# Last layer of a four-layer graph network: one two-bank PSUM tile for the turned factors, one bank for the side work

## The chip, the core and the metric

The kernel runs on one core of one Trainium2 chip. The metric is the device time of one execution in microseconds, as the median of several runs. TensorE (PE), VectorE (DVE), ScalarE (ACT), GpSimd (POOL) and SyncE (SP, which here only issues transfers) run side by side, each through its own queue in order; semaphores tie them together. PE writes its results into PSUM, of which each of 128 partitions has eight banks of 512 fp32 numbers. A tile of `[128, 512]` fp32 fills one bank.

## The reference

`x` is 4096 x 64, `adj` is 4096 x 4096. Four layers follow one another, each as `x = layernorm(x + layer(x, adj, ...))`: a Chebyshev layer, an attention layer with two GRU cells, a layer with decaying weights of the last neighbours of each row, and a layer in the Poincare ball. The change lies in the last one, with the curvature 1:

```python
def _logmap(x, y, c):
    sub = _mobius_add(-x, y, c)
    sub_norm = jnp.maximum(jnp.linalg.norm(sub, axis=-1, keepdims=True), MIN_NORM)
    x2 = jnp.sum(x * x, axis=-1, keepdims=True)
    lam_x = 2.0 / jnp.maximum(1.0 - c * x2, MIN_NORM)
    sqrt_c = jnp.sqrt(c)
    arg = jnp.clip(sqrt_c * sub_norm, 0.0, TANH_CLIP)
    return 2.0 / (sqrt_c * lam_x) * jnp.arctanh(arg) * sub / sub_norm
...
deg = jnp.maximum(adj.sum(axis=1, keepdims=True), 1e-08)
w = adj / deg
log_ij = _logmap(x[:, None, :], x[None, :, :], c)
agg = jnp.einsum('ij,ijc->ic', w, log_ij)
transformed = agg @ weight + bias
return _expmap(jnp.zeros_like(transformed), transformed, c)
```

For each pair of rows i, j the layer needs one factor f(i, j), a function of the distance of the two points, by which the adjacency is multiplied before it is summed against the features. The factor is the same for (i, j) and (j, i).

## The kernel before

The 4096 rows form 8 groups of 512. Because f is symmetric, the last layer computes it only for 36 tiles of 512 x 512, `tiles = [(i, j) ...]`, ordered by group `i` along a list `seq`: the first group has 8 tiles, the next 7, and so on down to 1. The first tile of a group is its diagonal tile. The adjacency, turned, lies in DRAM as `adj_t`; for each tile SP loads `own[t]` (the block at (i, j), buffer `at_d`) and, off the diagonal, `mirrored[t]` (the block at (j, i), buffer `at_m`), three buffers each.

Each tile is done in two halves, called units: `n` counts 72 of them (`NU`), each with 2 blocks of 128 x 512, so 128 x 1024 numbers; on the diagonal the second half is only 256 columns wide a block. The loop `while n < NU + 2` is written as a pipeline over units. In step `n` it does, in this written order:

- `gather(...)` (L1665, L1677, L1673): PE sums finished blocks of an `own` and of a `mirrored` tile against the features into `sums_ps`, one bank; a group's sums are then copied to `tb`.
- `turn(...)`: PE transposes the factors of a finished tile (L1649) for its mirrored block, four transposes of 128 x 128 into one PSUM tile `post`, and DVE multiplies each such tile into a block of `mirrored[t]` (L1651). A half has two blocks, so two `post` tiles and two multiplies. Turns of one tile are spread over two steps. A diagonal tile is turned onto itself (L1642, L1644), written at the end of its step (`late_turns`).
- ACT takes a logarithm (L1837) and an exponential (L1838) of unit `n`, the square of unit `n+1` (L1606), another exponential (L1864) and a logarithm of unit `n-1` (L1873). PE adds the sign part, `opposite(n + 1)` (L1616).
- DVE forms `f` for unit `n-2` (L1847) and multiplies it into `own` (L1850), then the multiplies of `turn`, then `rt` of unit `n` out of the product's PSUM banks (L1862), then `less_one(n + 1)` (L1627).
- PE forms `product(n + 2)` (L1594) into the two banks that L1862 has just read. Even units use pool `ps_v`, odd ones `ps_u`, two banks each.
- One step of `seam`: side work cut into pieces. At first it ends the layer before (`summed` L1389, `prepare`, `turn_prepared`); later it ends a finished group (`finals`): `first` forms products with `tb` (L1757), read by DVE (L1759) and ACT (L1767); `second` forms others (L1730), read by DVE (L1771); then normalisation and the store.
- `right(ps_p, i)`: PE forms the right side of a new group's products in two ways (L1356), four matmuls each into a `post` tile, and ACT copies each out (L1359). The second group's right side is formed at step 0; each later one six steps before the group's first unit, both ways in one step, into one of two buffers in turn.

All `post` tiles of the layer, those of `turn`, `seam` and `right`, come from one pool, `ps_p3`, of three banks. With the two banks each of `ps_v` and `ps_u` and the one of `sums_ps` that makes all eight.

What orders the work: a scheduler places each engine's instructions by the order in which they are written and by when their inputs are expected; an instruction may be drawn forward past others that wait. `in_order(ins)` forbids this for one instruction: it stays behind the instruction written just before it on its engine. The matmuls of `gather`, `opposite` and `product` are held in this way; the transposes and the side work are not. So the last transpose of a step stays ahead of the next `opposite`, and the last side matmul of a step ahead of the next `gather`. A tile of a pool can be written again only when every reader of its bank's former tile has ended.

Of the kernel before, what the change touches and what calls it, by code (L numbers as in the profile page):

```python
# [9 lines left out]
F32 = mybir.dt.float32  # L10
# [5 lines left out]
ALU = mybir.AluOpType  # L16
AX = mybir.AxisListType
PSUM = bass.MemoryType.PSUM
# [42 lines left out]
def gnn4_kernel(  # L61
# [21 lines left out]
    nc = tc.nc  # L83
    P = 128
# [3 lines left out]
    GW = GB * P  # L88
# [40 lines left out]
    ident = const.tile([P, P], F32, name="ident")  # L129
# [80 lines left out]
    def cols(b):  # L210
        return slice(b * P, (b + 1) * P)
# [317 lines left out]
    with tc.tile_pool(name="acc", bufs=1) as acc_p, tc.tile_pool(  # L529
        name="cols0", bufs=4  # L530
    ) as cols_p, tc.tile_pool(name="kept0", bufs=1) as kept_p, tc.tile_pool(name="diag0", bufs=2) as diag_p, tc.tile_pool(
        name="ps_t0", bufs=3, space=PSUM
    ) as ps_t, tc.tile_pool(name="ps_a0", bufs=1, space=PSUM) as ps_a, tc.tile_pool(
        name="ps_p0", bufs=2, space=PSUM
# [178 lines left out]
        for g in range(NG):  # L713
# [3 lines left out]
            for c in reversed(range(NCH)):  # L717
# [5 lines left out]
                for k in range(CB):  # L723
                    jb = c * CB + k
                    tp = ps_t.tile([P, GW], F32, name="tp", tag="tp")
# [37 lines left out]
                n = g * NCH + c  # L763
# [75 lines left out]
        due, n = [], 0  # L839
# [34 lines left out]
    tr_c = tr_x  # L874
# [9 lines left out]
    seq = turns_of[0] + turns_of[1]  # L884
# [371 lines left out]
    for signed in (False, True):  # L1256
        with cmp.Else() if signed else tc.If(all_positive > 0) as block:
            cmp = block
            with tc.tile_pool(name="cols1", bufs=3 if not signed else 2) as cols_p, tc.tile_pool(name="sign1", bufs=1) as sg, tc.tile_pool(
                name="tail1", bufs=1  # L1260
            ) as tl, tc.tile_pool(name="ps_a1", bufs=1, space=PSUM) as ps_a, tc.tile_pool(
                name="ps_p1", bufs=2, space=PSUM
# [7 lines left out]
    tr_o = some[:, 0 : N // 4].bitcast(BF16).rearrange("p (m n) -> p m n", n=P)  # L1270
# [76 lines left out]
    rights, begun = {}, {}  # L1347
    rvs = [some[:, N // 4 + q * GW : N // 4 + (q + 1) * GW] for q in range(2)]
    ros = [wq_signed.rearrange("p q h -> p (q h)")[:, 0 : GW // 2].bitcast(BF16)]

    def right(ps_p, i):
        q = seq.index(i) % 2
        for to, w, t in ((rvs[q], to_right, tr_c), (ros[q], to_other, tr_o)):
            ps = ps_p.tile([P, GW], F32, name="post", tag="post")
            for b in range(GB):
                nc.tensor.matmul(  # L1356
                    ps[:, cols(b)], lhsT=w[:, b % 2, :], rhs=t[:, (i * GB + b) // 2, :], start=True, stop=True
                )
            nc.scalar.copy(to, ps)  # L1359
        rights[i] = rvs[q], ros[q]  # L1360
# [65 lines left out]
    with tc.tile_pool(name="mask2", bufs=3) as mk_p, tc.tile_pool(name="wt2", bufs=3) as wt_p, tc.tile_pool(  # L1426
        name="ps_c2", bufs=1, space=PSUM
# [28 lines left out]
        gathers = []  # L1456
        busy = True
        for turn, groups in enumerate(turns_of):
            cnt = [ps_c.tile([P, GW], F32, name=f"cnt_ps{a}") for a in range(2)]
            if turn:  # L1460
                acc = [ps_a.tile([P, GW], F32, name=f"acc_ps{q}") for q in range(QG)]
                to_right, to_other, spread, wh_x = constants3()
# [5 lines left out]
            for h in reversed(range(2 * NB)):  # L1468
                jb, odd = divmod(h, 2)
                c, k = divmod(jb, CB)  # L1470
# [66 lines left out]


    with tc.tile_pool(name="ps_v3", bufs=1, space=PSUM) as ps_v, tc.tile_pool(
        name="ps_p3", bufs=3, space=PSUM  # L1540
    ) as ps_p, tc.tile_pool(name="ps_u3", bufs=1, space=PSUM) as ps_u, tc.tile_pool(name="o3", bufs=1) as op, tc.tile_pool(name="cols3", bufs=3) as cols_p, tc.tile_pool(
        name="w3", bufs=4
    ) as wp3, tc.tile_pool(name="el3", bufs=3) as el, tc.tile_pool(name="f3", bufs=2) as fp, tc.tile_pool(
        name="r3", bufs=2
    ) as rp, tc.tile_pool(
        name="ps_a3", bufs=1, space=PSUM
    ) as ps_a:
        HB = CB // 2
# [6 lines left out]
        tiles = [(i, j) for n, i in enumerate(seq) for j in seq[n:]]  # L1555
        NT = len(tiles)
        own, mirrored = {}, {}
# [4 lines left out]
        def load_own(t):  # L1562
            if t < NT and t not in own:
                i, j = tiles[t]
                own[t] = cols_p.tile([P, CB, GW], F32, name="at_d", tag="atd")
                nc.sync.dma_start(own[t], adj_t[i][:, j * CB : (j + 1) * CB, :])

        def load_mirrored(t):
            if t < NT and t not in mirrored and tiles[t][0] != tiles[t][1]:
                i, j = tiles[t]  # L1570
                mirrored[t] = cols_p.tile([P, CB, GW], F32, name="at_m", tag="atm")
                nc.sync.dma_start(mirrored[t], adj_t[j][:, i * CB : (i + 1) * CB, :])

        def columns(n):

            i, j = tiles[n // 2]
            return slice(2 * P if i == j and n % 2 else 0, GW)

        sums, fs = {}, {}
        ros.append(op.tile([P, GW], BF16, name="ro1"))  # L1580
        vs, ws, rts = {}, {}, {}
        NU = 2 * NT
# [18 lines left out]
        def square(n):  # L1601
            if n >= NU:
                return
            ws[n] = wp3.tile([P, HB, GW], F32, name="w3")
            cs = columns(n)
            nc.scalar.activation(ws[n][:, :, cs], vs[n][:, :, cs], AF.Square)  # L1606
# [26 lines left out]
        def turn(n):  # L1633

            t, h = n
            i, j = tiles[t]
            work = []
            if i == j:
                tp = ps_p.tile([P, GW], F32, name="post", tag="post")
                for k in range(HB):  # L1640
                    for b in range(HB):
                        nc.tensor.transpose(tp[:, cols(HB * k + b)], fs[t][:, b, cols(HB + k)], ident)  # L1642
                to = own[t][:, HB:CB, 0 : HB * P]
                work.append(lambda: nc.vector.tensor_tensor(to, tp.rearrange("p (k i) -> p k i", k=HB), to, ALU.mult))  # L1644
                return work
            for b in (HB * h, HB * h + 1):
                tp = ps_p.tile([P, GW], F32, name="post", tag="post")
                for k in range(CB):
                    nc.tensor.transpose(tp[:, cols(k)], fs[t][:, k, cols(b)], ident)  # L1649
                to = mirrored[t][:, b, :]  # L1650
                work.append(lambda to=to, tp=tp: nc.vector.tensor_tensor(to, tp, to, ALU.mult))  # L1651
            return work

        def gather(t, h, tm):
# [78 lines left out]
        def ahead_of_last(g):  # L1733
            def step(ps_p):
                turned_x[g] = rp.tile([P, GB, F], F32, name="xw")
                nc.scalar.copy(turned_x[g], weighed_x(ps_p, g))
                zs[g] = less_last(g)

            return step
# [71 lines left out]
            return [nothing, first, second, third, fourth, fifth]  # L1811

        seam += [weights, factors]
        turns, late_turns, gathers = {}, {}, {}

        for t in range(3):
            load_own(t)
# [6 lines left out]
        n = 0  # L1824
        while n < NU + 2 or turns or gathers:
            if n % 2:
                load_own((n + 1) // 2)
                load_mirrored((n - 1) // 2)
            after = gather(*gathers.pop(n)) if n in gathers else []
            turned = [w for what in turns.pop(n, []) for w in turn(what)]  # L1830
            if n < NU:
                if n % 2 == 0:
                    fs[n // 2] = fp.tile([P, CB, GW], F32, name="f3")
                w, cs = ws[n][:, :, columns(n)], columns(n)
                rts[n] = el.tile([P, HB, GW], F32, name="rt3")
                rt = rts[n][:, :, cs]
                nc.scalar.activation(w, w, AF.Ln)  # L1837
                nc.scalar.activation(rt, w, AF.Exp, scale=0.5)  # L1838
                square(n + 1)
                opposite(n + 1)  # L1840
            if n >= 2 and n - 2 < NU:
                m = n - 2
                t, h = divmod(m, 2)
                cm = columns(m)
                hs = slice(h * HB, (h + 1) * HB)
                f, at = fs[t][:, hs, cm], own[t][:, hs, cm]
                nc.vector.scalar_tensor_tensor(  # L1847
                    f, rts.pop(m)[:, :, cm], T_MAX, ws.pop(m)[:, :, cm], ALU.min, ALU.mult
                )
                nc.vector.tensor_tensor(at, at, f, ALU.mult)  # L1850
                diagonal = tiles[t][0] == tiles[t][1]
                before = t - 1 if t and tiles[t - 1][0] != tiles[t - 1][1] else None
                gathers[n + 1] = (t, h, before)
                if diagonal and h == 0:
                    late_turns[n + 1] = (t, 0)
                if not diagonal and h == 1:
                    turns.setdefault(n + 1, []).append((t, 0))
                    turns.setdefault(n + 2, []).append((t, 1))
            for work in turned:
                work()  # L1860
            if n < NU:
                nc.vector.scalar_tensor_tensor(rt, vs[n][:, :, cs], (1.0 + V_FLOOR) * SCALE, rt, ALU.max, ALU.add)  # L1862
                product(n + 2)
                nc.scalar.activation(w, w, AF.Exp, scale=-0.5)  # L1864
            late = turn(late_turns.pop(n)) if n in late_turns else []
            for work in after:
                work()
            less_one(n + 1)
            for work in late:
                work()  # L1870
            if 0 < n <= NU:
                rt = rts[n - 1][:, :, columns(n - 1)]
                nc.scalar.activation(rt, rt, AF.Ln, scale=1.0 / SCALE)  # L1873
            if n == NU - 6:
                seam += [ahead_of_last(g) for g in seq[-2:]]
            for _ in range(2 if n == 0 else 1):
                if seam:
                    seam.pop(0)(ps_p)
            if n == 0:
                right(ps_p, seq[1])  # L1880
            if n + 6 < NU and tiles[(n + 6) // 2][0] not in rights:
                i = tiles[(n + 6) // 2][0]
                right(ps_p, i)
            n += 1

        before, last = seam[:-6], seam[-5:]
# [49 lines left out]
```

## Time and profile before

| | |
|---|---|
| median of 3 runs | 1389.8 us (1385.99 to 1391.12) |
| the profiled execution | 1390.6 us, span 1388.5 us |
| busy over the span | PE 1298.1 us, DVE 1041.6 us, ACT 807.1 us, POOL 115.0 us |
| last layer's loop | first product at 959.7 us, last gather at 1367.7 us |
| DVE multiplies of turned factors, L1651 | 112 of 128x512, 74.4 us |
| transposes for them, L1649 | 448 |
| mean granted PE clock | 0.985 of full speed |

A profile names each group of instructions by its line, engine and operation, with the tile that it writes and the tiles that it reads (`at_m<-post,at_m`), partitions x elements, and a count. `SCALAR_TENSOR_TENSOR` and `TENSOR_TENSOR` are DVE operations with one and two whole tensors beside a scalar or none. PE does an fp32 matmul in two passes, so that such a matmul shows as two records, while an fp32 transpose shows as one. "idle before" is time in which the engine stood still just ahead of the group, with what ended the wait. The share of busy time is an average over the layers, so the last layer has to be read by itself.

### The profile page before, as it was taken

How to read it: one execution, taken by the hardware profiler on the slowest of the kernel's cores; microseconds unless marked ns; L12 is line 12 of the kernel's file. 1: busy time of each engine (PE TensorE's matmuls, PEld its weight loads, DVE VectorE, ACT ScalarE, POOL GpSimd, SP SyncE). 2: the span in 40 equal slices, each digit the busy share in tenths (PEclk: the TensorE clock that was granted, in tenths of full speed). 3: DMA queues.
4: the chain of work that ended last, by engine and by line, in shares of the span. 5: the costliest groups of instructions: out<-in, count | busy, mean ns of one | idle time of the engine just before them, and what ended most of it. 6: DMA issues, size and time to landing. Idle time of an engine off the chain costs nothing.

```text
span 1388.5 us, 19040 instructions
## 1 busy us (share of the span) xinstructions
PE 1298.1 (93%) x6790; PEld 607.6 (44%) x6790; DVE 1041.6 (75%) x1952; ACT 807.1 (58%) x1345; POOL 115.0 (8%) x200
## 2 busy tenths in 40 slices
PE   7999999999999999999999999998978888989893
PEld 5656566565544334444444323333333333333341
DVE  6699989999434257787886233436999999999997
ACT  4645444444000115654423675655989999999994
POOL 3111111101123000010101000001000000000000
PEclk9999999999999999999999999999999999999997
DMA  9999999999799999999885755453344454544430
GB/s 322 398 395 415 405 412 413 416 397 392 284 386 368 391 424 363 421 366 346 310 326 179 236 184 182 139 167 127 116 182 182 155 207 180 193 156 182 156 126 11
DMA packets 108190, 382.15 MB, mean 275 GB/s; under 512 B 20276, under 2 KB 20280, under 8 KB 76472
## 3 DMA queue, kind: packets, MB, share of 16 engines
q1 hardware_dynamic: 87096, 296.17, 58.0%
q0 software_dynamic: 12736, 76.29, 13.3%
q10 hardware_dynamic: 8256, 8.39, 1.7%
q8 instruction: 56, 0.92, 0.3%
q14 instruction: 46, 0.38, 0.1%
HBM read 294.05 MB, written 85.20 MB: 273 GB/s over the span
## 4 chain that ended last, share of the span: by engine, by line
PE 59%; ACT 18%; DVE 14%; DMA 6%; issue 2%; ACTq 0%; DVEq 0%; SPq 0%
PE pass L570 7%; PE tp L727 6%; PE w_ps L570 4%; PE a_last L1186 4%; PE pass L563 4%; PE cnt_ps L1477 4%; DMA raw<-in_adj_dram 4%; PE acc_ps L1437 4%; PE a_ps L1186 4%; PE h_ps L563 3%; ACT w L1837 3%; ACT w L1606 3%; ACT rt L1838 3%; ACT rt L1873 3%; PE wide_last L1177 2%; ACT wt L1482 2%
## 5 line engine op out<-in xcount | busy, mean ns | idle before, releaser
L734 ACT COPY at<-tp 128x512 f32<-128x512 f32 x248 | 128.1, 599 | 117.9 <-issue 90.1
L1482 ACT ACTIVATE wt<-cnt_ps 128x512 uint16<-128x512 f32 x212 | 117.5, 596 | 63.6 <-PE cnt_ps L1477 61.3
L762 DVE TENSOR_REDUCE dpart<-raw 128x4 f32<-128x2048 f32 x64 | 145.4, 2273 | 4.4 <-DMA raw<-in_adj_dram 4.3
L1665 PE MATMUL sums_ps<-at_d,some 128*64 128x512 f32 x288 | 145.1, 625 | 2.8 <-ACT tb L1684 1.1
L764 DVE TENSOR_REDUCE lows<-raw 128x1 f32<-128x2048 f32 x64 | 145.4, 2272 | 0.0
L727 PE MATMUL tp<-ident,raw 128*128 128x128 f32 x1024 | 131.9, 282 | 6.5 <-DMA raw<-in_adj_dram 5.5
L727 PEld LDWEIGHTS tp<-ident,raw 128*128 128x128 f32 x1024 | 115.9, 144 | 42.8 <-issue 32.6
L1677 PE MATMUL sums_ps<-at_m,some 128*64 128x512 f32 x224 | 109.4, 610 | 0.0
L1594 PE MATMUL v_ps<-some,tr_a 64*128 64x512 f32 (+1 forms) x288 | 79.1, 626 | 22.7 <-DVE rt L1862 21.9
L570 PE MATMUL pass<-at,cheb_n 128*128 128x512 f32 x224 | 97.5, 593 | 0.5 <-DVE cheb_n L796 0.5
L570 PE MATMUL w_ps<-at,cheb_n 128*128 128x512 f32 x200 | 91.1, 598 | 0.0
L1477 PE MATMUL cnt_ps<-m,follow 128*64 128x512 fp8e4 x480 | 81.9, 391 | 5.4 <-ACT wt L1482 2.2
L1862 DVE SCALAR_TENSOR_TENSOR rt<-v_ps,rt 128x1024 f32<-128x1024 f32 x72 | 83.1, 1155 | 2.2 <-PE post L1649 1.2
L1850 DVE TENSOR_TENSOR at_d<-at_d,f 128x1024 f32<-128x1024 f32 x72 | 83.4, 1158 | 0.1
L1847 DVE SCALAR_TENSOR_TENSOR f<-rt,w 128x1024 f32<-128x1024 f32 x72 | 83.1, 1154 | 0.4 <-ACT rt L1873 0.3
L1649 PE MATMUL post<-ident,f 128*128 128x128 f32 x448 | 69.3, 284 | 8.5 <-DVE at_m L1651 4.2
L1873 ACT ACTIVATE rt<-rt 128x1024 f32<-128x1024 f32 x72 | 72.3, 1004 | 8.4 <-DVE rt L1862 8.0
L1484 DVE TENSOR_SCALAR wt<-cnt_ps 128x512 uint16<-128x512 f32 x44 | 30.4, 691 | 61.8 <-PE cnt_ps L1477 61.8
L1651 DVE TENSOR_TENSOR at_m<-post,at_m 128x512 f32<-128x512 f32 x112 | 74.4, 679 | 2.7 <-PE post L1649 2.6
L1837 ACT ACTIVATE w<-w 128x1024 f32<-128x1024 f32 x72 | 71.8, 999 | 1.7 <-DVE w L1627 1.5
L1864 ACT ACTIVATE w<-w 128x1024 f32<-128x1024 f32 x72 | 72.4, 1006 | 0.7
L1838 ACT ACTIVATE rt<-w 128x1024 f32<-128x1024 f32 x72 | 72.4, 1005 | 0.5
(425 smaller groups left out, 2270.2 us busy)
## 6 DMA issues: line engine op xcount, KB each, us to landing
at<-adj_t SPq DMA_DIRECT2D x119, 1024.0 KB, 7.8
raw<-in_adj_dram SPq DMA_DIRECT2D x64, 1024.0 KB, 12.7
adj_t<-at POOLq DMA_DIRECT2D x62, 1024.0 KB, 8.3
at_d<-adj_t SPq DMA_DIRECT2D x36, 1024.0 KB, 4.7
at_m<-adj_t SPq DMA_DIRECT2D x28, 1024.0 KB, 6.7
m<-mask_t SPq DMA_DIRECT2D x120, 128.0 KB, 2.8
m<-mask_t SPq DMA_DIRECT2D x60, 256.0 KB, 4.1
mask_t<-mask ACTq DMA_DIRECT2D x28, 256.0 KB, 7.6
```

The lines of the kernel that those rows point to most:

```text
L570: in_order(nc.tensor.matmul(ps, lhsT=cheb_n[:, jb, k : k + 2, :], rhs=rhs, start=first, stop=last))
L727: in_order(nc.tensor.transpose(tp[:, cols(b)], raw[:, b, cols(k)], ident))
L734: nc.scalar.copy(at[:, k, :], tp)
L762: in_order(nc.vector.tensor_reduce(dpart[:, g, c, :], raw, AX.X, ALU.add))
L764: in_order(nc.vector.tensor_reduce(lows[:, n : n + 1], raw.rearrange("p b j -> p (b j)"), AX.X, ALU.min))
L1186: in_order(nc.tensor.matmul(ps[q * F : (q + 1) * F, :], lhsT=nat_a[:, c * CB + k, 0:F], rhs=of[q if signed else 0][:, k, :], start=(c == 0 ...
L1477: in_order(nc.tensor.matmul(cnt[a][r * HP : (r + 1) * HP, :], lhsT=follow, rhs=chunks[c][odd][2 * a + r][:, k, :], start=(h == 2 * NB - 1) ...
L1482: in_order(nc.scalar.activation(wt[odd][a], cnt[a], AF.Relu, scale=-128.0))
L1665: in_order(nc.tensor.matmul(bank[0:F, :], lhsT=nat_c[:, j * CB + k, :], rhs=own[t][:, k, :], start=(i == j and k == 0), stop=(j == seq[-1] ...
L1837: nc.scalar.activation(w, w, AF.Ln)
L1838: nc.scalar.activation(rt, w, AF.Exp, scale=0.5)
L1873: nc.scalar.activation(rt, rt, AF.Ln, scale=1.0 / SCALE)
```

## The change

The pool `ps_p3` goes from three banks to one, and a new pool `ps_t3` of two banks is opened, with one buffer. In `turn`, the two `post` tiles of a half become one tile of `[128, 2, 512]` in that pool; the eight transposes go into it, and one multiply over 128 x 1024 takes the place of two over 128 x 512. Everything else that used `post` in this layer (diagonal turns, `seam`, `right`) now shares the one bank of `ps_p3`. `right` gets an argument that says which of its two ways to form, and in the loop the first way is formed seven steps and the second six steps before the group's first unit.

```diff
-    def right(ps_p, i):
+    def right(ps_p, i, which=(0, 1)):
         q = seq.index(i) % 2
-        for to, w, t in ((rvs[q], to_right, tr_c), (ros[q], to_other, tr_o)):
+        for to, w, t in [((rvs[q], to_right, tr_c), (ros[q], to_other, tr_o))[m] for m in which]:
             ps = ps_p.tile([P, GW], F32, name="post", tag="post")
...
-        name="ps_p3", bufs=3, space=PSUM
-    ) as ps_p, tc.tile_pool(name="ps_u3", bufs=1, space=PSUM) as ps_u, ...
+        name="ps_p3", bufs=1, space=PSUM
+    ) as ps_p, tc.tile_pool(name="ps_t3", bufs=1, space=PSUM) as ps_t, tc.tile_pool(
+        name="ps_u3", bufs=1, space=PSUM
+    ) as ps_u, ...
...
-            for b in (HB * h, HB * h + 1):
-                tp = ps_p.tile([P, GW], F32, name="post", tag="post")
+            tp = ps_t.tile([P, HB, GW], F32, name="two_turned")
+            for b in range(HB):
                 for k in range(CB):
-                    nc.tensor.transpose(tp[:, cols(k)], fs[t][:, k, cols(b)], ident)
-                to = mirrored[t][:, b, :]
-                work.append(lambda to=to, tp=tp: nc.vector.tensor_tensor(to, tp, to, ALU.mult))
+                    nc.tensor.transpose(tp[:, b, cols(k)], fs[t][:, k, cols(HB * h + b)], ident)
+            to = mirrored[t][:, HB * h : HB * h + HB, :]
+            work.append(lambda: nc.vector.tensor_tensor(to, tp, to, ALU.mult))
             return work
...
-            if n + 6 < NU and tiles[(n + 6) // 2][0] not in rights:
-                i = tiles[(n + 6) // 2][0]
-                right(ps_p, i)
+            for m, way in ((7, 0), (6, 1)):
+                if n + m < NU:
+                    i = tiles[(n + m) // 2][0]
+                    if (i, way) not in halves and i != seq[1] and i != seq[0]:
+                        halves.add((i, way))
+                        right(ps_p, i, (way,))
```

## The prediction

> **What bounds the kernel now.** The span table places the change first: everything it touches lies between the first product of the last layer (959.7 us) and the tail (from 1370 us). So I read the busy time of each engine in stretches of that layer; the columns are length, then busy time and instruction count of PE, PEld, DVE, ACT and POOL, PE clock, DMA share, GB/s.
>
> ```profile
> 1000.00:1050.00 50.00, 41.77 (x192) 16.80 (x189) 49.40 (x82) 43.68 (x49) 0.00 (x0) 0.93 0.42 161
> 1050.00:1100.00 50.00, 43.22 (x215) 18.74 (x214) 48.83 (x77) 49.04 (x72) 1.56 (x2) 1.00 0.45 165
> ...
> 1200.00:1250.00 50.00, 45.19 (x218) 18.74 (x217) 48.09 (x76) 48.97 (x74) 1.56 (x2) 1.00 0.48 180
> ...
> 1300.00:1350.00 50.00, 47.83 (x242) 21.69 (x240) 48.51 (x81) 49.76 (x82) 1.56 (x2) 1.00 0.43 154
> ```
>
> Over all seven stretches from 1000 to 1350 us DVE is busy 336.5 us and ACT 336.5 us of 350: both 96%. PE has 87% at first and 96% in the last stretch. DMA has half its time left and decides nothing here. So two engines bound the loop together, and a third joins them late, where the groups are short.
>
> Second the groups of that layer, shapes kept apart (count | busy us, mean ns | idle before):
>
> ```profile
> L1862 DVE SCALAR_TENSOR_TENSOR rt<-v_ps,rt 128x1024 f32<-128x1024 f32 x64 | 77.7, 1214 | 2.2 <-PE post L1649 1.2 <-ACT rt L1838 0.7
> L1651 DVE TENSOR_TENSOR at_m<-post,at_m 128x512 f32<-128x512 f32 x112 | 74.4, 679 | 2.7 <-PE post L1649 2.6
> L1649 PE MATMUL post<-ident,f 128*128 128x128 f32 x448 | 69.3, 284 | 8.5 <-DVE at_m L1651 4.2 <-DVE f L1847 4.1
> ```
>
> The multiplies to be joined hardly wait (2.7 us in 112); the transposes that feed them wait more. The waits of that stretch say for what (total us, times, longest):
>
> ```profile
> PE v_ps L1594 <- DVE rt L1862: 21.9, 25, 3.5
> ...
> PEld post L1649 <- DVE at_m L1651: 10.1, 18, 1.3
> ACT rt L1873 <- DVE rt L1862: 8.0, 15, 1.9
> DVE w L1627 <- ACT w L1606: 7.5, 8, 1.8
> ```
>
> PE's main pause is before a product, which needs the bank pair that `rt` (L1862) reads. That pause is where PE now does work early. The timeline at the turn of a group shows it:
>
> ```profile
> 1213.53 0.66 PE L1642 MATMUL post<-ident,f 128*128 128x128 f32 x4
> 1214.02 1.06 PE L1757 MATMUL post<-two_w,tb 128*128 128x128 f32 x8
> 1214.91 1.00 PE L1730 MATMUL post<-wh_x,tr_a 128*128 128x64 f32 x8
> 1215.42 0.68 DVE L1644 TENSOR_TENSOR at_d<-post,at_d 128x512 f32<-128x512 f32 x1
> 1215.84 1.13 PE L1594 MATMUL v_ps<-some,tr_a 64*128 64x512 f32 x4
> 1216.90 0.64 PE L1665 MATMUL sums_ps<-at_d,some 128*64 128x512 f32 x1
> 1217.09 0.90 ACT L1767 ACTIVATE v<-post,kappa 128x64 f32<-128x64 f32 x4
> ```
>
> Three side results (a diagonal tile's turn L1642, and two steps of the previous group's end, L1757 and L1730) stand in three `post` banks at once, before the first is read at 1215.42.
>
> **The change part by part.** Durations are from the profiled execution: 1390.6 us, a span of 1388.5 and 2.1 around it. It lies 0.8 us over the median of the three runs, 1389.8, to which I add the sum.
>
> *A, one multiply for two.* 112 multiplies of 128x512 become 56 of 128x1024. By busy time: 74.4 us against 56 x 1.214 = 68.0 us (the nearest row, L1862, also reads one PSUM operand of 128x1024), 6.4 us less. By starts in the timeline: two multiplies back to back take 1.28 us (at 1213.09) and one of 1024 takes 1.21 to 1.22, so 56 x 0.07 = 3.9 us less. How much reaches the end? ACT is as busy as DVE and loses no work, so what leaves DVE mostly turns into waiting on ACT; I take half of the smaller figure, **-2 us**; ends -6.4 and 0.
>
> The Trainium skill (Perfetto Trace Analysis, section Optimizing Scalar/DVE Operations) puts the fixed cost of a DVE operation on PSUM at about 125 ns and says that grouping helps when the engine is saturated; by it 56 operations fewer would be worth 7.0 us, an estimate, against the 3.9 us of the starts above. The same section says that breaking instructions up may finish work sooner where DVE is not saturated and makes other engines wait, which speaks against this change.
>
> *B, eight transposes into one double bank.* Until now a multiply could start after four transposes (a block of four is 0.66 us) and the third bank let the next four go ahead. Now a multiply needs eight (one block of eight at 1268.91 us took 1.09 us), 0.43 us more, and the next eight cannot begin until the whole multiply has ended. Behind the last of them PE holds, in its written order, the opposite product (L1616) and then the product (L1594); behind the multiply DVE holds `rt`, and the next step's gather waits for the multiply too. Because the gather already needs the multiply, transposes placed after it never wait for the bank. Upper end: the 0.43 us in full on each of 56 halves, +24 us. Lower end: the 2.6 us that DVE waits for `post` now go away, -2.6 us. The nearest row is that small wait, so I stay near it: one half in six pays, 56/6 x 0.43 = **+4 us**.
>
> *C, one bank for the side.* At the six group ends inside the loop where both side steps follow a diagonal turn, L1757 must wait until L1644 has read the bank (1216.10 at the place shown), and L1730 until the four activations at L1767 are through (1217.99). Of PE's work 1.06 + 1.00 = 2.06 us leaves a pause that exists anyway and comes later, and the first matmul of the next gather is written behind it. The six places cost at most 6 x 2.06 = 12.4 us. The two formed halves of a new right side (L1356) are now one step apart, so a step forms one of them; but for two of the six new groups the earlier half falls into the very step of a diagonal turn and L1757, the later one into that of L1730. There a block of 1.16 us and a copy of 0.58 us (L1359) line up behind the rest: 2 x 1.74 = 3.5 us. Upper end +15.9. Lower end: L1730 holds up the product by 0.35 us at the place shown (its block ends 1215.91, `rt` was free at about 1215.5); without it 6 x 0.35 = 2.1 us are gained. PE idles some 10% before 1300 us and only 4% after, so it regains part: **+5 us**, a third of the upper end. If the bank waits are hidden by that slack and the slack is gone, as after 1300 us, the part is paid in full.
>
> The same skill page, section Optimizing Tensor Performance, Matmuls, says that independent groups should rotate through different banks so that reading one overlaps forming the next; the three blocks above do so now, and read strictly the rule would put all of the upper end, +15.9 us, on the clock, which would make the sum +18 us, an estimate.
>
> *D, edges, one answer each.* The right side at step 0 now follows the DVE add of the step before it in the same bank (964.68 + 0.69 us, against a start at 964.48): 0.9 us later, hidden, since the next product waits for `rt` until 967.47. At the tail the two last groups' L1757 stand together (16 passes, 2.05 us at 1369.86); now the second waits for the first to be read (about 1371.9) and takes 1.03 us, but its reader starts only at 1373.88: 0, at most 0.5. The earlier half of the last right side overwrites a buffer whose last product is written in the same step, 1.13 us if ACT meets that copy too soon: taken as 0. The diagonal turn keeps its form. SP's and POOL's queues are passed by nothing: no DMA is moved, and `tb` and the mirrored tiles are loaded as before.
>
> Sum: -2 + 4 + 5 = +7, so 1389.8 + 7 = **1397 us**.
>
> **The rivals.**
> *The shorter DVE path wins (not slower).* If all eight transposes fit into PE's pause between a multiply and the end of the following `rt` (1.13 us net, block of eight 1.09), B and C are nothing and A counts: 1389.8 - 3.9 to 1389.8 - 6.4 = 1383.4 to 1385.9; with the lower ends of B and C, 1378.7. For it: PE waits 21.9 us before products now. Against it: at the turns of groups that pause is already used. It decides if B and C together stay below 3.9 us, 0.07 us a half.
>
> *PE's written order becomes the loop.* Where DVE takes the multiply before `rt` and the next eight transposes were not drawn forward, a step is a ring: multiply 1.21, `rt` 1.21, product 1.13, gather 1.93 (1205.58 to 1207.51), transposes 1.09, together 6.57 us. The products at 1199.82 and 1220.41 us are four steps apart, 5.15 us a step. So 1.42 us for each half it happens to; for a quarter of 56, +20, 1410 us; for all, +80. Against it: DVE may take `rt` first, and then the ring opens.
>
> *Nothing moves.* Both engines stay at 96%, the freed 4 us are lost in waits of the same size: 1388 to 1392.
>
> **How the numbers follow.** Forecast (+2 to +15 us, own range 1392 to 1405): 0.42, since its two places are seen in the rows; nothing moves 0.22; DVE path wins 0.22; ring 0.14. A measurement of this kernel tells about 0.5%, 6.9 us. Faster by more needs under 1382.9, the better part of the DVE rival's span: 0.10. Slower by more: three quarters of the forecast and the ring, 0.32 + 0.14 = 0.46. The rest, 0.44, is within. The range 1383 to 1411 leaves out 0.10 below and about 0.09 above (half of the ring, the forecast's end).
>
> **What would show it.** Right: 56 multiplies of 128x1024 near 1.21 us; DVE's share in 1050 to 1300 falls by about 1% while ACT's does not rise; waits of the L1649 transposes on the multiply grow beyond 14 us; the blocks L1757 and L1730 start after L1644 and L1767. Wrong: transposes of eight regularly standing before the product, with DVE idle before the multiply still near 3 us (DVE rival), or idle before L1862 and L1651 over 20 us (ring). The forecast fails as a whole if the work comes out in another order on PE, so that the pauses before products change in number: they are 21.9 us, three times the sum.

## The result and the profile after

The changed kernel takes 1402.6 us (median of 6 runs, 1401.04 to 1405.0) against 1390.1 us for the kernel before (6 runs, 1385.99 to 1394.09): a ratio of 1.0094, 95% interval 1.0079 to 1.011. It is slower by about 12.5 us. The profiled execution has a span of 1400.5 us.

The time is lost inside the loop of the last layer. From the first `rt` operation to the 72nd (L1862 before, L1864 after: the line numbers of the loop move by two) the profiled executions take 390.2 us (966.26 to 1356.44) and 404.4 us (964.01 to 1368.44), 14.2 us more. What follows the last one takes 32.1 us in both, and the first comes 2.3 us earlier, so nothing is lost ahead of the loop.

The busy time of each engine in stretches of the changed kernel, with the columns as before (length, then PE, PEld, DVE, ACT, POOL, PE clock, DMA share, GB/s):

```profile
1000.00:1050.00 50.00, 39.53 (x185) 15.69 (x185) 47.39 (x71) 43.44 (x48) 0.00 (x0) 0.97 0.43 168
1050.00:1100.00 50.00, 43.77 (x210) 19.97 (x210) 48.13 (x67) 46.76 (x70) 1.03 (x2) 0.97 0.43 163
...
1200.00:1250.00 50.00, 44.89 (x202) 20.30 (x202) 44.50 (x65) 44.28 (x67) 2.11 (x2) 0.90 0.44 168
...
1300.00:1350.00 50.00, 45.14 (x227) 20.32 (x226) 48.20 (x80) 48.39 (x79) 1.56 (x2) 1.00 0.41 150
sum 350.00, PE 305.74 PEld 131.34 DVE 326.32 ACT 325.98 POOL 7.85; mean PE 43.68 PEld 18.76 DVE 46.62 ACT 46.57 POOL 1.12
```

The sum over the same seven stretches of the kernel before was:

```profile
sum 350.00, PE 310.93 PEld 131.31 DVE 336.50 ACT 336.49 POOL 7.82; mean PE 44.42 PEld 18.76 DVE 48.07 ACT 48.07 POOL 1.12
```

DVE and ACT, which bound the loop together, each stand still 10 us more in these 350 us. Neither has taken the other's place: both wait. The stretch from 1200 to 1250 us is the worst, and PE's clock is lowered there to 0.90 on average, where it was 1.00 before.

The groups of the layer, shapes apart (count | busy us, mean ns | idle before):

```profile
L1864 DVE SCALAR_TENSOR_TENSOR rt<-v_ps,rt 128x1024 f32<-128x1024 f32 x64 | 78.0, 1218 | 4.8 <-ACT rt L1840 2.7 <-ACT tb L1686 1.7
...
L1653 DVE TENSOR_TENSOR at_m<-two_turned,at_m 128x1024 f32<-128x1024 f32 x56 | 68.4, 1221 | 10.7 <-PE two_turned L1651 10.3
...
L1651 PE MATMUL two_turned<-ident,f 128*128 128x128 f32 x448 | 66.2, 284 | 16.4 <-DVE at_m L1653 13.1 <-DVE f L1849 3.2
```

The joined multiplies are 6.0 us less busy than the 112 before (74.4), but DVE waits 10.7 us ahead of them, 8.0 us more. The waits of the loop, in us in total, times and longest:

```profile
PEld two_turned L1651 <- DVE at_m L1653: 17.9, 14, 2.3
...
PE v_ps L1618 <- ACT w L1608: 12.3, 17, 2.2
ACT rt L1875 <- DVE rt L1864: 12.2, 16, 1.6
DVE at_m L1653 <- PE two_turned L1651: 10.3, 10, 3.5
...
ACT tb L1686 <- PE sums_ps L1679: 8.7, 6, 2.8
```

The timeline at the same turn of a group as before (the fourth) shows what became of the side work:

```profile
1216.06 0.44 PE L1644 MATMUL post<-ident,f 128*128 128x128 f32 x2
...
1218.12 0.68 DVE L1646 TENSOR_TENSOR at_d<-post,at_d 128x512 f32<-128x512 f32 x1
...
1218.35 1.31 PE L1596 MATMUL v_ps<-some,tr_a 64*128 64x512 f32 x4 [1.85 <-DVE rt L1864]
...
1219.58 2.07 PE L1759 MATMUL post<-two_w,tb 128*128 128x128 f32 x8
...
1222.22 0.93 ACT L1769 ACTIVATE v<-post,kappa 128x64 f32<-128x64 f32 x4
...
1223.20 2.08 PE L1356 MATMUL post<-tr_a,to_right 128*128 128x128 f32 x8 [1.12 <-ACT v L1769]
...
1225.20 1.12 PE L1667 MATMUL sums_ps<-at_d,some 128*64 128x512 f32 x1
...
1230.27 1.10 PE L1732 MATMUL post<-wh_x,tr_a 128*128 128x64 f32 x8
```

Before, three blocks stood in three banks inside PE's pause. Now PE stands idle 1.85 us ahead of the product, L1759 comes after the diagonal turn's multiply, a right side (L1356) after the four activations that read L1759's bank, and only then the gather, written behind it. L1759 takes 2.07 us where it took 1.06 and each pass of the gather 1.06 to 1.12 instead of 0.59: the PE clock. In windows of 5 us (columns as above) it reads:

```profile
1215.00:1220.00 5.00, 3.15 (x18) 1.61 (x17) 4.63 (x6) 5.00 (x6) 0.00 (x0) 0.92 0.16 66
1220.00:1225.00 5.00, 3.88 (x18) 3.46 (x17) 4.30 (x7) 3.78 (x8) 2.11 (x2) 0.50 0.01 2
1225.00:1230.00 5.00, 5.00 (x16) 1.38 (x14) 3.27 (x4) 2.87 (x5) 0.00 (x0) 0.56 0.06 13
1230.00:1235.00 5.00, 4.75 (x28) 2.66 (x28) 5.00 (x8) 4.86 (x6) 0.00 (x0) 1.00 0.97 390
```

In the two windows at half the clock DVE and ACT are busy 7.6 and 6.7 us of 10. That is a single group end: from the 45th `rt` (1209.49 us) to the 52nd (1255.7) the changed kernel's lag behind the kernel before, counted from the first `rt`, grows from 4.5 to 9.3 us, of 14.2 in the whole loop. It is one of the two group ends at which the earlier half of a right side falls into the same step, so it need not be typical.

### The profile page after: what moved, and what is told of

Its sections match the earlier page's. It is cut to its first block, busy times and chain, and to the rows that moved or that the text cites. A ratio compares the mean times of both kernels' runs of the same rounds, so it can differ in the third digit from the quotient of the medians.

```text
span 1400.5 us, 18990 instructions
## 1 busy us (share of the span) xinstructions
PE 1299.8 (93%) x6790; PEld 609.4 (44%) x6790; DVE 1040.8 (74%) x1896; ACT 807.8 (58%) x1345; POOL 115.2 (8%) x200
## 4 chain that ended last, share of the span: by engine, by line
PE 63%; ACT 13%; DVE 12%; DMA 8%; issue 2%; SPq 1%; ACTq 0%; POOL 0%; DVEq 0%
PE pass L570 7%; PE tp L727 7%; DMA raw<-in_adj_dram 6%; PE w_ps L570 5%; PE pass L563 4%; PE cnt_ps L1477 4%; PE a_last L1186 4%; PE a_ps L1186 4%; PE h_ps L563 4%; PE acc_ps L1437 3%; PE sums_ps L1667 3%; DVE rt L1864 3%; PE wide_last L1177 2%; ACT w L1839 2%; PE p_ps L1177 2%
## 5 line engine op out<-in xcount | busy, mean ns | idle before, releaser
L727 PEld LDWEIGHTS tp<-ident,raw 128*128 128x128 f32 x1024 | 112.9, 141 | 47.6 <-issue 35.1
L1679 PE MATMUL sums_ps<-at_m,some 128*64 128x512 f32 x224 | 113.1, 627 | 0.0
L1864 DVE SCALAR_TENSOR_TENSOR rt<-v_ps,rt 128x1024 f32<-128x1024 f32 x72 | 83.4, 1158 | 4.9 <-ACT rt L1840 2.7
L1651 PE MATMUL two_turned<-ident,f 128*128 128x128 f32 x448 | 66.2, 284 | 16.4 <-DVE at_m L1653 13.1
L1653 DVE TENSOR_TENSOR at_m<-two_turned,at_m 128x1024 f32<-128x1024 f32 x56 | 68.4, 1221 | 10.7 <-PE two_turned L1651 10.3
L1651 PEld LDWEIGHTS two_turned<-ident,f 128*128 128x128 f32 x448 | 48.7, 142 | 57.8 <-issue 28.7
```

What stands on the lines that cost most here:

```text
L727: in_order(nc.tensor.transpose(tp[:, cols(b)], raw[:, b, cols(k)], ident))
L1651: nc.tensor.transpose(tp[:, b, cols(k)], fs[t][:, k, cols(HB * h + b)], ident)
L1679: in_order(nc.tensor.matmul(bank[F:P, :], lhsT=nat_c[:, above * GB + k, :], rhs=mirrored[tm][:, k, :], start=(k == 0 and above == seq[0]), ...
```

## The experiments

All ratios are against runs of the kernel before on the same chip, with 95% intervals. "Clock lost" is worked out from each profile in windows of 5 us: the sum of 5 x (1 - granted clock) from 1040 to 1355 us. The column leaves out the start of the layer: from 960 us on, the sums are 8.6 for the kernel before, 13.7 for the change, 6.8 for diagonal_apart and 13.7 for split_right_alone. Every edit lets the scheduler lay out the whole loop anew, so each ratio holds the edit together with the order of work that it brought.

| kernel | ratio to before | clock lost, us |
|---|---|---|
| before | 1 | 0 |
| the change | 1.0094 (1.0079 to 1.011) | 8.5 |
| side_one_bank | 1.0048 (1.0032 to 1.0064) | 11.9 |
| two_multiplies | 1.0116 (1.0094 to 1.0139) | 13.7 |
| diagonal_apart | 0.9998 (0.9987 to 1.0009) | 0 |
| dve_relief_alone | 0.9993 (0.9981 to 1.0005) | 5.1 |
| singles_diagonal_apart | 1.0019 (1.0008 to 1.003) | 1.8 |
| pauses_filled | 1.0071 (1.0056 to 1.0086) | 1.4 |
| first_step_later | 1.0124 (1.0106 to 1.0142) | 8.6 |
| right_together | 1.0058 (1.0042 to 1.0075) | 1.8 |
| apart_and_together | 1.0041 (1.0024 to 1.0059) | 5.1 |
| right_in_two | 1.0079 (1.0061 to 1.0097) | 5.1 |
| split_right_alone | 0.9987 (0.9973 to 1.0) | 6.8 |
| before_filled | 0.9992 (0.9976 to 1.0007) | 1.8 |

My theory was that the single side bank costs most (C), the coarser turn less (B), and that little of DVE's relief arrives (A). The rival was the joined turn itself, by waiting or by PE's order.

### The side bank without the joining

```diff
-            tp = ps_t.tile([P, HB, GW], F32, name="two_turned")
-            for b in range(HB):
+            for b in (HB * h, HB * h + 1):
+                tp = ps_t.tile([P, GW], F32, name="one_turned")
...
-name="ps_t3", bufs=1
+name="ps_t3", bufs=2
```

> The change without the joining: the side work keeps its one bank and its split right sides, the turns get two tiles of one bank each and two multiplies of 128x512 as before. If the single side bank is what costs (part C, +5 us estimated), this is about 1395 us, with the 112 multiplies at 74.4 us. If the joined turn is what costs (part B), this is within 3 us of before, 1390. If the ring in PE's order alone costs, it is near 1390 too.

Measured: 1.0048. Half of the loss is there although the 112 multiplies stand as before. So the rival, that the joining alone does it, falls. But 0.48%, or 6.7 us, is not the whole 0.94%: on top of the single side bank, joining the turns adds the other half, 6.4 us, and these two intervals do not overlap.

### Two multiplies out of the two-bank tile

```diff
-            to = mirrored[t][:, HB * h : HB * h + HB, :]
-            work.append(lambda: nc.vector.tensor_tensor(to, tp, to, ALU.mult))
+            for b in range(HB):
+                to = mirrored[t][:, HB * h + b, :]
+                work.append(lambda to=to, b=b: nc.vector.tensor_tensor(to, tp[:, b, :], to, ALU.mult))
```

> The changed kernel with the two-bank tile kept, but read by two multiplies of 128x512, each after its own four transposes. It takes back the gain of part A (3.9 us more of DVE) and the 0.43 us of waiting for the second four. If waiting for eight transposes is the cost, it is 3 to 8 us faster than the changed kernel (1402.6), near 1397. If the tile's release as a whole or the side bank is the cost, it is equal or up to 4 us slower, 1402 to 1407.

Measured: 1.0116, no gain and if anything a loss of some 3 us against the change (the intervals overlap). Starting a multiply after four transposes rather than eight brings nothing, and DVE's idle time ahead of the multiplies hardly falls (9.1 us instead of 10.7). So nothing here shows waiting for the second four as the cost; the run also lost more of PE's clock (13.7 against 8.5 us), which it does not separate. The Trainium skill (Perfetto Trace Analysis, Optimizing Scalar/DVE Operations) says that breaking instructions up may finish work sooner where an engine is not saturated and causes bubbles elsewhere; here, with DVE busy 93% of the main stretch, it did not.

### The diagonal turn out of the side bank

```diff
-                tp = ps_p.tile([P, GW], F32, name="post", tag="post")
+                tp = ps_t.tile([P, HB, GW], F32, name="two_turned")[:, 0, :]
                 for k in range(HB):
                     for b in range(HB):
                         nc.tensor.transpose(tp[:, cols(HB * k + b)], ...)
```

> The changed kernel with the diagonal tile's turn moved out of the side bank into the two-bank tile (one of its banks). If the side bank's line of users at a group's end is a main cost (part C), it gives back 2 to 6 us: 1397 to 1400. If the joined turn is the cost, it stays at 1402 or becomes slower, since the diagonal turn now waits for the multiply of the turn before it.

Measured: 0.9998. One line, eight diagonal turns, and the whole loss is gone (in the profiled executions 12.3 of the loop's 14.2 us), twice the gain that I had expected at most. The timeline of the same group end shows why:

```profile
1212.69 0.66 PE L1644 MATMUL two_turned<-ident,f 128*128 128x128 f32 x4
...
1213.19 1.06 PE L1759 MATMUL post<-two_w,tb 128*128 128x128 f32 x8
...
1217.03 1.16 PE L1356 MATMUL post<-tr_a,to_right 128*128 128x128 f32 x8 [0.38 <-ACT v L1769]
...
1221.17 1.11 PE L1732 MATMUL post<-wh_x,tr_a 128*128 128x64 f32 x8
```

L1759 directly follows the diagonal turn inside PE's pause, as it did before, and no block takes 2 us. In 1210 to 1240 us this profile's PE clock is 1.00 in every window of 5 us. DVE's wait for turned blocks falls with it, although the multiplies are still joined. The first line is the whole loop, where the changed kernel had 10.7 us of idle time and the kernel before 2.7; the second is 1000 to 1350 us, where the wait was 5.3 us in the changed kernel and 1.8 before:

```profile
L1653 DVE TENSOR_TENSOR at_m<-two_turned,at_m 128x1024 f32<-128x1024 f32 x56 | 68.2, 1218 | 3.3 <-PE two_turned L1651 3.1
...
DVE at_m L1653 <- PE two_turned L1651: 2.2, 3, 1.3
```

So most of those waits went away with the queue for the side bank, and not with the joining.

### DVE's relief alone

```diff
-                to = mirrored[t][:, b, :]
-                work.append(lambda to=to, tp=tp: nc.vector.tensor_tensor(to, tp, to, ALU.mult))
+                to = mirrored[t][:, b, 0:478]
+                work.append(lambda to=to, tp=tp: nc.vector.tensor_tensor(to, tp[:, 0:478], to, ALU.mult))
```

> The kernel before with each of the 112 multiplies cut from 512 to 478 columns; it leaves out the last 34 columns of each mirrored block's factor. That takes 112 x 35 ns = 3.9 us off DVE, the size of part A, and changes nothing else. By the prediction half of it reaches the end: -2 us, 1388. If ACT bounds the loop alone it is 1390; if DVE does, 1386.

Measured: 0.9993, or -1.0 us (-2.6 to +0.7). The 112 multiplies are busy 70.7 us in this profile against 74.4, so 3.7 us and not 3.9 were taken off one of two equally busy engines. They give at most 2.6 us, some 0.7 of that; half, as taken, lies inside, and so does nothing.

### Two single banks for the turns, diagonal turn among them

```diff
# against side_one_bank
-                tp = ps_p.tile([P, GW], F32, name="post", tag="post")
+                tp = ps_t.tile([P, GW], F32, name="one_turned")
```

> As side_one_bank (one side bank, two turned tiles of one bank, two multiplies), but the diagonal turn writes one of the turned tiles and not the side bank. If the diagonal turn in the side bank is the whole cost, this comes back to the time before, 1388 to 1392, as diagonal_apart did, and then joining the multiplies is worth less than 2 us. If the joined multiply had paid for other costs of the single side bank in diagonal_apart, this is 3 to 6 us slower than that one, 1392 to 1396.

Measured: 1.0019, against 1.0048 with the diagonal turn in the side bank. The same one-line move helps without the joining too, but by 4 us, where it gave 13 with the joined turns. Against diagonal_apart, 0.9998, the joined multiply in a two-bank tile is worth about 0.2%, 3 us; the intervals touch, so this is likely and not shown.

### Pauses filled

```diff
-                for k in range(HB):
-                    for b in range(HB):
-                        nc.tensor.transpose(...)
+                for _ in range(4):
+                    for k in range(HB):
+                        for b in range(HB):
+                            nc.tensor.transpose(...)
```

> The changed kernel with the four transposes of each diagonal turn formed four times over into the same tile, same values: 12 more transposes, some 1.3 us of PE work, at each of the eight turns, where PE stands still before the next product. If the lower PE clock that follows those pauses is the cost, the clock stays at 1.00 through 1200 to 1300 us and the time falls to 1392 to 1398 in spite of the added work. If only the order of the bank's users costs, the time stays at 1402 or rises by up to 8 x 1.3 = 10 us.

Measured: 1.0071. The clock lost falls from 8.5 to 1.4 us and the time by about 3 us in spite of 96 more transposes; the intervals of 1.0071 and 1.0094 overlap. The net gain is about a quarter of the loss. It is no upper limit of what the clock costs, because here the added transposes also hold up the next user of the single side bank: at the fourth turn the diagonal block takes 1.97 us (0.66 for its four alone), and L1760, which is L1759 of the changed kernel, starts only after it has been read. At that place the queue stands at full clock: the right side (L1356) still waits 1.88 us for the activations.

### The same filling in the kernel before

The edit is the same, made in the kernel before.

> The control to pauses_filled: the kernel before, with the same 12 added transposes at each of the eight diagonal turns. Between 1040 and 1355 us its PE clock is not lowered, so there is nothing to restore. If the gain of pauses_filled (3.3 us against the changed kernel) came from the clock, the added work gains nothing here: equal or up to 10 us slower, 1390 to 1400. If more transposes in that place are good in themselves, by another order of the work, this is faster than before by 2 us or more.

Measured: 0.9992, no change. In this kernel, with three side banks, the added transposes cost nothing measurable and bring nothing by themselves. That agrees with the clock as the reason for the 3 us, as far as those are real.

### The group's end one step later

```diff
-            return [nothing, first, second, third, fourth, fifth]
+            return [nothing] * (2 if g in seq[:5] else 1) + [first, second, third, fourth, fifth]
```

> The changed kernel with the first and second steps of a finished group's end (L1759, L1732) each written one step later for the first five groups, so that the step of the diagonal turn has no other user of the side bank than that turn (and in one group a right side). If the pair diagonal turn and L1759 in one step is the cost, this falls to 1390 to 1395. If the diagonal turn alone, waiting for the bank, is the cost, it stays above 1398.

Measured: 1.0124, slower still. Of the two outcomes that I had written down, the first, that the pair of diagonal turn and L1759 in one step is the cost, did not come; the second, above 1398 us, did. It does not show the diagonal turn alone as the cost, though: the timeline at the fourth turn shows that the queue only changed its members there:

```profile
1224.57 2.07 PE L1356 MATMUL post<-tr_a,to_right 128*128 128x128 f32 x8
...
1230.20 1.16 PE L1759 MATMUL post<-two_w,tb 128*128 128x128 f32 x8
...
1234.78 0.59 PE L1356 MATMUL post<-some,to_other 128*128 128x128 bf16 x4 [2.55 <-ACT v L1769]
```

Now the first way of the right side follows the diagonal turn, and the second way shares the step of L1759 and waits 2.55 us for the activations that read it. By the step numbers in the kernel the right side meets the diagonal turn at two of the six group ends only, so this place does not explain the loss at the other four.

### Both ways of a right side in one step

```diff
-            for m, way in ((7, 0), (6, 1)):
+            for m, way in ((6, 0), (6, 1)):
```

> The changed kernel with both ways of a right side formed in one step again, six steps ahead, through the one side bank. The prediction counted two blocks of 1.74 us lining up: if the second way has to wait for ACT's copy inside its step, six groups lose 1 to 1.7 us each, 1407 to 1413. If the pause is hidden by other work, it is within 3 us of 1402.6.

Measured: 1.0058. The split of the right sides, part of the change, costs about 5 us in this kernel, and these intervals do not overlap. I had expected the opposite. At the group end shown, the seven-step half is what falls into the step of a diagonal turn and L1759; put back, it stands behind L1732 in the next step (at 1222.55 us), and the second way waits only 0.54 us for ACT's copy.

### The split alone, with three banks

The edit is the change's own part for `right`, made in the kernel before.

> The kernel before, three side banks and two multiplies, with the two ways of a right side formed seven and six steps ahead. If a step of both ways or one matters in itself, this differs from before by the 5 us that right_together showed. If it matters only through the single bank, where the earlier way falls into the step of a diagonal turn, it equals before within 2 us.

Measured: 0.9987 (0.9973 to 1.0). Where three banks are to be had, the split costs nothing. The 5 us belong to the kernel with the single bank.

### Both reliefs together, and the right sides in the two-bank tile

apart_and_together has the edits of diagonal_apart and right_together. right_in_two adds to diagonal_apart:

```diff
+        two = ps_t.tile([P, 2, GW], F32, name="two_turned")
+        for m, (to, w, t) in enumerate(((rvs[q], to_right, tr_c), (ros[q], to_other, tr_o))):
...
+            nc.scalar.copy(to, two[:, m, :])
```

> diagonal_apart and right_together in one kernel: the diagonal turn in the two-bank tile, both ways of a right side in one step six ahead. If the two edits relieve the side bank in the same place, this equals diagonal_apart, 1388 to 1391. If they add up, 5 us less than that, 1383 to 1386, and it beats both kernels.

> diagonal_apart with both ways of a later right side formed into the two banks of a turned tile in one step, so that the side bank serves the group ends and the layer's start alone. If the side bank is still crowded in diagonal_apart, this gains 1 to 4 us, 1385 to 1388. If the turned tile is the scarcer one, held by ACT's two copies ahead of the next turn, it loses 2 to 6 us, 1391 to 1395.

Measured: 1.0041 and 1.0079. Neither beats diagonal_apart. The two reliefs do not add up: the edit that gained 5 us in the changed kernel costs 6 us here. In the profiles apart_and_together keeps step with diagonal_apart up to the 63rd unit (0.4 us behind it) and loses 3 us and more in the last short groups, where DVE waits 3.06 us for one turned block (at 1348.74 us). right_in_two loses steadily from the middle on, as expected of a turned tile that is held by ACT's copies. Why the last groups of apart_and_together suffer is not settled: no run here separates the edit from the new order of work.

No version was found that beats both kernels; diagonal_apart equals the kernel before.

## Why the prediction came out as it did

The forecast was 1397 us, slower, in a range of 1383 to 1411; measured were 1402.6. The direction held, and so did the places: a longer wait ahead of the multiplies and a queue for the side bank at a group's end. The size did not. The prediction priced its parts one by one and added them; the runs show that B and C are not separate.

- **A, one multiply for two: -2 us.** By busy time the multiplies became 6.0 us less, near the 6.4 us that the prediction had by this count. By starts a joined one holds DVE for 1.13 us (1210.62 to 1211.75) against 1.20 us for a pair before (1213.09 to 1214.29), again the 0.07 us a half that the prediction used. What a relief of 3.7 us of busy time gives, measured alone, is 1.0 us (-2.6 to +0.7). That agrees with the step that DVE's gain mostly turns into waiting on ACT, and is too wide to show it.
- **B, eight transposes into one double bank: +4 us.** What the joined turn costs depends on C. With the diagonal turn in the side bank, A and B together add 6.4 us (1.0094 against 1.0048), where the forecast had +2. With the diagonal turn apart they add nothing (0.9998 against 1.0019), and DVE stands idle 3.3 us ahead of the multiplies instead of 10.7. Two multiplies out of the same tile do not help either. At one place transposes of eight did stand ahead of a product while `rt` ran (eight at 1196.16 us, the product at 1197.29), as the rival of the faster DVE path had supposed.
- **C, one bank for the side: +5 us.** Alone it was sized about rightly: side_one_bank, with single turned tiles, loses 6.7 us (4.4 to 8.9). The step that failed is the sum, which adds B and C as if each stood alone. Taking the diagonal turn out of the side bank gives back 4 us with single turned tiles and 13 us with the joined one, so some 9 us belong to the two together, and no term of the prediction held that. Why they make each other dearer is not settled. At the place shown, the step "PE idles some 10% before 1300 us and only 4% after, so it regains part" (12% by the rows) did not hold: the next gather, product and turn stand behind the pause that PE loses at the group's end, and both bounding engines then wait. There PE's clock was lowered too, which the prediction did not count at all: the three blocks between 1219.58 and 1228.9 us (L1759, L1356, the gather) took some 3.6 us longer than at full clock (1.0 + 0.9 + 1.7).
- **The split right sides** were counted as lining up in two of six groups, 3.5 us; right_together shows 5 us. The place was right, and I then expected the reverse when I wrote down right_together. That the size comes near is partly luck: in diagonal_apart the same edit has the opposite sign.
- **The signs.** The waits of the transposes on the multiply grew, as forecast, from 10.1 and 4.2 us (weight loads and matmuls) to 17.9 and 13.1. But diagonal_apart has 18.6 and 10.5 and loses nothing, so this sign does not tell a loss from none. DVE's share from 1050 to 1300 us fell by 3.1 points, not 1, and ACT's, which was to stay, by 3.6: both engines wait.
- **D, the edges: 0.** What follows the last `rt` takes 32.1 us in both profiles, so the tail is untouched. No DMA queue shows in the new waits.
- **The rivals.** The DVE path did not win: B and C together, some 13 us with A at about -1, are far above 3.9 us. The ring did not form: the waits ahead of L1864 and L1653 together are 15.5 us, under the 20 us named. "Nothing moves" is what the one-line move of the diagonal turn restores.

## What to carry to other kernels

A buffer that is shared by rare, irregular users has to be counted at the step where most of them meet, in the written order of the engine that fills it, and not by its average use: here the gather of the whole loop stood behind the last side block of a step. When banks are taken from a shared pool to make one operation larger, look first which user can move into the new tile's idle time; here one user moved made the difference of 13 us, and only 4 us where the turned tiles were single. So the price of a shared bank depends on what else was changed with it: two changes of the same step are measured one by one and together, and their prices are not simply added. And where two engines were equally busy here, making one of them faster was worth little, while a pause of the third one kept both waiting.

## What the runs showed of the hardware

PE's clock was not flat at the pauses. After idle times of 1.85 us at 1218 and 1279 us in the changed kernel it was lowered, to 0.50 in the worst window, with matmul passes of 1.06 us instead of 0.59, their starts 0.86 us apart instead of 0.43. But a pause of 1.81 us at 1185.92 us in the same profile left it at 1.00, and 1.89 us at 1182.26 us in diagonal_apart did too; the length of the pause alone does not tell. The Trainium skill (TensorE: Matmul & The Clock Gate, Part 1) says that the clock has two states, full and half, decided over free-running windows of about 3.4 us; the half state agrees with the 0.50 and the doubled distance of the starts, and windows that run freely would explain why equal pauses end differently, but no run here shows the windows.

A lowered clock need not cost time: split_right_alone lost 6.8 us of clock and dve_relief_alone 5.1, and neither was slower than the kernel before, while the changed kernel lost 8.5 and was (from 960 us on, split_right_alone and the changed kernel even lose the same 13.7). That the loss counts only where PE is the one awaited would explain this; no run here tests it.
